# Node weights of a graph layer: slots of 16 outputs with both halves of the supports, in three bursts, for slots of 32 outputs with one half, in four periods

## The chip, the cores and the metric

The kernel runs on one core of one Trainium2 chip. The metric is the time of one execution on the device in microseconds. Before the change it is 1736.24 us, the median of three runs (1735.61 to 1749.89).

TensorE (PE) multiplies, and a weight load (PEld) goes before each matmul; its results go to PSUM[...]. VectorE (DVE) and ScalarE (ACT) read PSUM. [...]SyncE (SP) issues most DMA transfers, each engine in its own program order.

## The reference, cut to what matters

Four graph layers follow one another on x (8 batches, 2048 nodes, 64 features), each with a residual and a layernorm. The change is in the third, where every node has weights of its own, made from an embedding of 16 numbers:

```
support_set = [eye(N), lap, 2 * lap @ lap - eye(N), apt]         # lap is adj here
weights = einsum('nd,dkio->nkio', node_embeddings, weights_pool)  # 4 supports x 64 in x 64 out for every node
bias = node_embeddings @ bias_pool
x_g = einsum('knm,bmc->bknc', supports, x)                        # transposed to b, n, k, c
out = einsum('bnki,nkio->bno', x_g, weights) + bias
```

The fourth layer multiplies with adj again, three times.

## The kernel before, in words

Supports times x are formed first (`supports()`), transposed, and stored to DRAM as four terms: xt, u1, u2, u3. While they run, small jobs of the list `aside` are done one per tile step: among them 8 of the 16 adjacency tiles are written to `adj_hbm` (`keep_adj`), since their SBUF (`more0`, `more1`, 4 tiles or 4 MB each) is lent to the node weights; and the weight pool, split[...], is prepared as two stacks `wst[0]`, `wst[1]`, one for each half (two supports, 128 rows) of the contraction.

Then come the slots. A chunk is 256 nodes (8 chunks). For a chunk, `load_unit` brings two tiles `xg`, one for each half k: 1 MB as two DMAs (line 1440). A slot g stands for a chunk c, a half of the outputs (`hf`, 32 of 64), and one half k of the contraction: 32 slots, 4 for each chunk.

- `form(g, s)`, eight in a slot, forms weights of 4 outputs for all 256 nodes: four fp32r matmuls `pw<-est,wst`, 64 rows by 128 columns of the array in two row tiles, 256 columns moved. ACT copies `pw` out of a tile of two banks (even s, line 1512), or ACT and DVE each copy one bank (odd s, line 1516) into `w_half[k]`.
- `multiply(g - 1, v)`, four in a slot, takes the weights formed in the slot before: for 4 nodes at a time a weight load of 128 rows by 32 columns (8 batches of 4 nodes) and a product with 128 columns (4 nodes of 32 outputs), four column tiles side by side: 16 fp32 matmuls, each of which the profile shows as two passes with a weight load each. The result holds products of each node with each of four nodes; `pick` (lines 1520 and 1522, DVE) keeps the diagonal with a mask, four picks of 128x256 for each pair of periods, after both halves k have been added up in PSUM.

A slot has four periods: two forms, up to two picks, then one multiply. The order on every engine is written out by this loop (`pin`, `tc.keep_in_program_order`). PSUM in the slots: two product tiles `py` of two banks ("ph"), one forming tile of two banks ("two") and two of one bank ("one"). The first slot's forms are done among the last matmuls of `supports()` (`opening_forms`); in the last slot there are only multiplies, and the first work for the fourth layer.

`hooks` put other steps at (slot, period): loads of `est` and of `xg` (three buffers that rotate), and `chunk_end`, eight steps that end a chunk: store of the sums to `y_hbm` and loads of the residual (`store`, line 1558), loads of y turned (`load`, 1570), sum, squares, power and scale (POOL, ACT, DVE), store to `x3_hbm`.

After the slots the lent tiles come back from `adj_hbm`, the first four by POOL's queue and the other four by SP's, behind the last chunk's store and load. `opening()` does the first product of the fourth layer: tiles 0 to 6 first, then 7 to 11, then 12 to 15; the last chunk's end is done beside it, and `first_turn(3)` (transposes `pt`, line 175) waits for it. Line 172 is the helper `mm` that all matmuls have, so groups are told apart by their tiles.

Of the kernel before, what the change touches and what calls it, by code (L numbers as in the profile page):

```python
# [56 lines left out]
def tile_gnn_fast(  # L57
# [181 lines left out]
    terms = [dram.tile([NP * P, N], F32, name=f"{name}_hbm") for name in ("xt", "u1", "u2", "u3")]  # L239
    xt_hbm, u1_hbm, u2_hbm, u3_hbm = ([a[p * P:(p + 1) * P, :] for p in range(NP)] for a in terms)  # L240
    est_hbm = dram.tile([P, N], F32, name="est_hbm")
    adj_hbm = dram.tile([8, P, N], F32, name="adj_hbm")
    wst_hbm = dram.tile([P, F // 2, P], F32, name="wst_hbm")
    y_hbm = dram.tile([N // 256, F, B, 4, F], F32, name="y_hbm")
    xb_hbm = dram.tile([NP, P, NT, P], F32, name="xb_hbm")
# [11 lines left out]
    def column_halves(a):  # L257
        return [a[:, cols(g, N // 2)] for g in range(2)]

    def lent_tiles():  # L260

        tiles = []
        for i in range(2):
            more = adj_pool.tile([P, LENT // 2, N], F32R, tag=f"more{i}", name="adj_more")
            tiles += [column_halves(more[:, k, :]) for k in range(LENT // 2)]
        return tiles

    adj = [adj_tile(adj_pool, t) for t in range(LEND)] + lent_tiles()

    hrows = {}  # L270

# [163 lines left out]
    with tc.tile_pool(name="pa_ps", bufs=1, space=PSUM) as pps:  # L435
# [215 lines left out]
        adj += [adj_tile(adj_end, t) for t in range(NT - XT, NT)]  # L651

        fetch_rows(0)
        fetch_rows(1)
# [584 lines left out]
    def supports():  # L1239

        for p in range(NP):
            for k, hbm in ((1, u1_hbm), (2, u2_hbm)):
                chunks = [2, 3, 0, 1] if p == 0 and k == 1 else [*range(NCH)]
                uts = {}
                for g in range(2):
                    own = (2 * g, 2 * g + 1)
                    closing = (p, k, g) == (NP - 1, 2, 1)
                    if closing:
                        chunks = [1, 2, 0, 3]
                    ug = pph.tile([P, 2, C], F32, tag="ph", name="u", bufs=2)  # L1250
                    for q in chunks:
                        for t in range(q * JT, (q + 1) * JT):
                            for i in range(2):
                                for c in own:
                                    mm(
                                        ug[:, c % 2, :], lhsT=x_part[q][i][:, t % JT, :], rhs=adj_c(t, c),
                                        start=t == chunks[0] * JT and i == 0,
                                        stop=t == chunks[-1] * JT + JT - 1 and i == 1,
                                    )
                                    tick()  # L1260
                                    yield
                            if closing and q == 2 and t % JT == JT - 2:
# [138 lines left out]
    def second_stack():  # L1401
        for q in range(8):
# [44 lines left out]

    def bank(name):
        if wps is not None:
            return wps.tile([P, 2, Q], F32, tag="one", name=name, bufs=2).rearrange("p o n -> p (o n)")  # L1450
        return lps.tile([P, C], F32, tag="mm", name=name, bufs=4)

    def first_h(p, c, h, kept=lambda i: i):
# [24 lines left out]
        h[c] = first_h(0, c, l2.tile([P, C], F32, tag=f"g{c}", name=f"h{c}"))  # L1478
        later(n, lambda: factor(c, h[c], bd_e, None))

    H = F // 2
    w_half, w_four, scopes = [], [], {}
    opening_forms = [*range(8)]

    def lend(i):
        w_half.append(adj_pool.tile([P, Q, H], F32, tag=f"more{i}", name="w_half"))
        w_four.append(w_half[i].rearrange("p (m n) o -> p n m o", m=4))

    def begin_slots():
        nonlocal wps  # L1490
# [4 lines left out]

    picks = []

    def form(g, s):

        (c, hf), k = divmod(g // 2, 2), g % 2  # L1500
        if s % 2 == 0:
            pw = wps.tile([P, 2, 2, Q], F32, tag="two", name="pw", bufs=1)
            banks = [pw[:, j] for j in range(2)]
        else:
            banks = [wps.tile([P, 2, Q], F32, tag="one", name="pw", bufs=2) for _ in range(2)]
# [4 lines left out]
        dst = w_half[k][:, :, 4 * s:4 * s + 4]  # L1510
        if s % 2 == 0:
            pin(nc.scalar.copy(dst, pw.rearrange("p j o n -> p n (j o)")))  # L1512
        else:
            for j, (bank, eng) in enumerate(zip(banks, (nc.vector, nc.vector if k and s > 3 else nc.scalar))):
                copy = eng.tensor_copy if eng is nc.vector else eng.copy
                pin(copy(dst[:, :, 2 * j:2 * j + 2], bank.rearrange("p o n -> p n o")))  # L1516

    def pick(dst, src, m, first):
        if first:
# [4 lines left out]
    for _ in filler:  # L1524
        pass
    assert not aside and not opening_forms
    second_stack()
    lend(1)
    sums_2 = xnp.tile([P, 2, O4, F], F32, tag="xn2", name="sums_2")
    py = {}  # L1530

    def multiply(g, v):

        (c, hf), k = divmod(g // 2, 2), g % 2
        if v % 2 == 0 and k == 0:
            py[v] = pph.tile([P, 2, 4, 4, H], F32, tag="ph", name="py", bufs=2)
        both = py[v - v % 2]
        for i in range(4):
            for j in range(4):
                n = O4 * j + 4 * v + i  # L1540
                mm(
                    both[32 * j:32 * (j + 1), v % 2, i], lhsT=xg[2 * c + k][:, n], rhs=w_four[k][:, n],
                    start=k == 0 and i == 0, stop=k == 1 and i == 3,
                )
        if v % 2 and k:
            dst = sums_2[:, c % 2, 4 * v - 4:4 * v + 4, hf * H:(hf + 1) * H]
# [69 lines left out]
        at(4 * c - 2, 0, lambda c=c: load_est(c))  # L1616
    ends = [chunk_end(c) for c in range(UNITS // 2)]
    for c, stages in enumerate(ends[:-1]):
        for (slot, period), f in zip(((5, 2), (5, 3), (7, 0), (7, 2), (7, 3), (8, 0), (8, 1), (8, 2)), stages):
# [13 lines left out]
    for q in range(2):  # L1633
        at(SLOTS, 1 + q, lambda q=q: factor(q, h[q], bd_e, None, True))

    for g in range(1, SLOTS + 1):
        for period in range(4):
            for f in hooks.pop((g, period), ()):
                f()
            if 0 < g < SLOTS:  # L1640
                form(g, 2 * period)
                form(g, 2 * period + 1)
            for f in picks[:2]:
                f()
            del picks[:2]
            if g > 0:
                multiply(g - 1, period)
            if g == SLOTS:
                for f in picks:
                    f()  # L1650
                picks.clear()
    store, load, *waiting = ends[-1]
    adj[LEND:LEND + LENT] = lent_tiles()
# [12 lines left out]
    scopes["w"].close()  # L1666
# [958 lines left out]
```

## Time and profile before

| what | value |
|---|---|
| median of three runs | 1736.24 us |
| the profiled execution, as timed | 1743.63 us |
| its span in the profile | 1741.8 us |
| granted TensorE clock in it | 0.987 |
| node-weight slots in the span | 1017.8 to about 1254 us |

From the page (groups by line, engine and tiles; x is the count, then busy us in total and the mean ns of one, then idle time of the engine before them and what ended it):

```profile
L1516 DVE COPY w_half<-pw 128x512 f32<-128x512 f32 x160 | 109.7, 705 | 86.2 <-PE pw L172 85.4
L1512 ACT COPY w_half<-pw 128x1024 f32<-128x1024 f32 x128 | 129.9, 1015 | 56.9 <-PE pw L172 56.8
...
L172 PE MATMUL py<-w_half,xg 128*32 128x128 f32 x4096 | 142.2, 279 | 1.2 <-issue 1.2
...
L172 PEld LDWEIGHTS py<-w_half,xg 128*32 128x32 f32 x4096 | 111.3, 138 | 18.8 <-issue 1.9
...
L172 PE MATMUL pw<-est,wst 64*128 64x256 f32 x1024 | 110.0, 317 | 0.7 <-ACT w_half L1512 0.4
```

"128*32" is the part of the array that is used, rows by columns. `<-issue` is idle time for which the profile shows no producer. Matmuls overlap, so the mean of one is longer than the distance between two.

### The profile page before, as it was taken

To read this page: it belongs to the slowest core of one execution; us is meant where nothing else is said; L and a number is where in the kernel's file an instruction comes from. 1 tells how busy PE (TensorE), PEld (TensorE's weight loads), DVE (VectorE), ACT (ScalarE), POOL (GpSimd) and SP (SyncE) were. 2 spreads that over 40 slices of the span, in tenths; PEclk is the share of its full clock that TensorE was granted. 3 is DMA by queue.
4 is the path that set the end of the run, shared out by engine and by line. 5 is a ranking of instruction groups with operands and counts; after the bars stand their busy time and mean duration, and the time that the engine had idled before them with its cause. 6 is when DMAs were issued, how large, how long until landed. Compare 5 with 4: busy or idle time off the path is not lost. (4 is left out here: it accounts for less than half of the span.)

```text
span 1741.8 us, 27973 instructions
## 1 busy us (share of the span) xinstructions
PE 1659.0 (95%) x11196; PEld 1208.1 (69%) x11196; DVE 833.1 (48%) x1531; ACT 589.4 (34%) x1031; POOL 572.4 (33%) x515
## 2 busy tenths in 40 slices
PE   6889899999989999999999999999989999999996
PEld 4657666666664444468788878888767877878775
DVE  7678945677742221210127247777623433433332
ACT  1345533434322211112123267878512222212221
POOL 4578845566534444422023001322310200202001
PEclk9899999999999999999999999999999999999998
DMA  9744334444340000017344367575671121211211
GB/s 336 252 158 124 107 123 145 139 147 132 107 151 6 30 7 24 25 54 291 120 143 124 109 152 159 131 171 123 157 265 43 51 59 43 61 48 42 57 43 39
DMA packets 171180, 195.83 MB, mean 112 GB/s; under 512 B 71536, under 2 KB 116336, under 8 KB 169760
## 3 DMA queue, kind: packets, MB, share of 16 engines
q1 hardware_dynamic: 160096, 154.54, 30.5%
q0 software_dynamic: 8544, 30.68, 5.3%
q10 hardware_dynamic: 2400, 8.72, 1.3%
q8 instruction: 90, 1.47, 0.4%
q14 instruction: 50, 0.41, 0.1%
HBM read 126.72 MB, written 67.17 MB: 111 GB/s over the span
## 5 line engine op out<-in xcount | busy, mean ns | idle before, releaser
L172 PE MATMUL ua<-pt,xn 128*128 128x512 f32 x512 | 230.2, 592 | 1.4 <-DVE pt L1151 1.4
L172 PEld LDWEIGHTS ua<-pt,xn 128*128 128x128 f32 x512 | 96.9, 190 | 111.1 <-issue 104.0
L1516 DVE COPY w_half<-pw 128x512 f32<-128x512 f32 x160 | 109.7, 705 | 86.2 <-PE pw L172 85.4
L1512 ACT COPY w_half<-pw 128x1024 f32<-128x1024 f32 x128 | 129.9, 1015 | 56.9 <-PE pw L172 56.8
L172 PE MATMUL py<-w_half,xg 128*32 128x128 f32 x4096 | 142.2, 279 | 1.2 <-issue 1.2
L172 PE MATMUL u<-adj,v0h 128*128 128x512 f32 x384 | 134.5, 428 | 1.1 <-ACT h L1820 1.1
L172 PE MATMUL u<-adj_more,v2h 128*128 128x512 f32 x384 | 126.1, 406 | 0.0
L172 PE MATMUL u<-adj,v0l 128*128 128x512 f32 x384 | 125.0, 403 | 0.0
L172 PEld LDWEIGHTS py<-w_half,xg 128*32 128x32 f32 x4096 | 111.3, 138 | 18.8 <-issue 1.9
L172 PE MATMUL u<-adj_more,v2l 128*128 128x512 f32 x384 | 124.3, 401 | 0.0
L1157 POOL TENSOR_TENSOR acc<-acc,pt 128x512 f32<-128x512 f32 x60 | 76.5, 1274 | 104.3 <-DVE pt L1151 103.6
L172 PE MATMUL pw<-est,wst 64*128 64x256 f32 x1024 | 110.0, 317 | 0.7 <-ACT w_half L1512 0.4
L1151 DVE TENSOR_SCALAR pt<-pt 128x512 f32<-128x512 f32 x64 | 29.9, 466 | 152.4 <-ACT pt L1150 152.3
L172 PEld LDWEIGHTS pw<-est,wst 64*128 64x128 f32 x1024 | 82.2, 184 | 25.6 <-ACT w_half L1512 18.4
L1729 ACT CAST ar<-fcav 128x512 fp32r<-128x512 f32 x64 | 39.6, 618 | 168.9 <-DMA fcav<-in_adj_t 168.0
L1730 DVE SCALAR_TENSOR_TENSOR ar<-fcav,ar 128x512 f32<-128x512 f32 x64 | 45.8, 715 | 102.4 <-ACT ar L1729 102.4
L172 PE MATMUL u<-adj_more,v3l 128*128 128x512 f32 x288 | 93.1, 399 | 1.2 <-DVE v3l L168 1.2
L172 PE MATMUL u<-adj,v1h 128*128 128x512 f32 x288 | 93.7, 403 | 0.0
L1150 ACT ACTIVATE pt<-s 128x512 f32<-128x512 f32 x64 | 38.0, 598 | 164.5 <-PE s L172 164.5
L172 PE MATMUL u<-adj_more,v3h 128*128 128x512 f32 x288 | 92.7, 400 | 0.0
L172 PE MATMUL u<-adj,v1l 128*128 128x512 f32 x288 | 92.0, 397 | 0.0
L1701 POOL TENSOR_TENSOR x<-x,rows 128x512 f32<-128x512 f32 x16 | 22.5, 1430 | 211.4 <-PE pt L175 127.8
(408 smaller groups left out, 3275.7 us busy)
## 6 DMA issues: line engine op xcount, KB each, us to landing
fcav<-in_adj_t SPq DMA_DIRECT2D x64, 256.0 KB, 3.0
u_hbm<-ut SPq DMA_DIRECT2D x48, 256.0 KB, 3.7
xg<-u_hbm SPq DMA_DIRECT2D x24, 512.0 KB, 7.7
adj<-in_adj_t POOLq DMA_DIRECT2D x16, 512.0 KB, 7.8
adj_more<-in_adj_t POOLq DMA_DIRECT2D x16, 512.0 KB, 9.8
adj_hbm<-adj_more SPq DMA_DIRECT2D x16, 512.0 KB, 6.2
x_hbm<-r SPq DMA_DIRECT2D x28, 256.0 KB, 2.3
hs_hbm<-st ACTq DMA_DIRECT2D x8, 584.0 KB, 4.8
```

What stands on the lines that cost most here:

```text
L172: tc.keep_in_program_order(nc.tensor.matmul(*args, **kw))
L1150: nc.scalar.activation(pt, s, AF.Exp)
L1151: nc.vector.tensor_scalar(pt, pt, 1.0, None, op0=ALU.max)
L1157: nc.gpsimd.tensor_tensor(accs[c], accs[c], pt, ALU.add)
L1512: pin(nc.scalar.copy(dst, pw.rearrange("p j o n -> p n (j o)")))
L1516: pin(copy(dst[:, :, 2 * j:2 * j + 2], bank.rearrange("p o n -> p n o")))
L1701: nc.gpsimd.tensor_tensor(xs, xs, b2.to_broadcast([P, JT, P]), ALU.add)
L1729: nc.scalar.copy(ar, seen_a)
L1730: nc.vector.scalar_tensor_tensor(ar.bitcast(F32), seen_a, 1.0, ar.bitcast(F32), op0=ALU.mult, op1=ALU.not_equal, accum_out=left[:, t, k:k ...
```

## The change

A slot now stands for a chunk and a quarter of the outputs (16), and has both halves k. `form(g, s)`: s counts 0 to 7, k = s // 4. `w_half[g % 2]` holds both halves of one slot; forms of a slot write one of them and multiplies of the slot before read the other. `multiply(g - 1, v, k)` moves 64 columns (4 nodes of 16 outputs) and is called 8 times a slot for 4. A product tile is one bank ("one", two of them); forming tiles are of two banks, three in turn (`two_banks`: "two", and two of "ph"), and each is copied whole, six of eight by ACT, two by DVE. A slot has three bursts: 3 forms and 3 multiplies, 3 and 3, 2 and 2.

`xg` gets a fourth buffer, in the place of the last adjacency tile, so this tile is also kept in `adj_hbm` (9 tiles for 8) and comes back last. Loads of `xg` are put at slots 4c - 2 and 4c - 1 for 4c - 3 and 4c. The second weight stack is loaded in pieces during the closing pass of `supports()`, since the opening forms need both stacks. The first four lent tiles return at the beginning of the last slot, by SP's queue.

```diff
-    adj_hbm = dram.tile([8, P, N], F32, name="adj_hbm")
+    adj_hbm = dram.tile([9, P, N], F32, name="adj_hbm")
...
+                            if closing and t % JT == JT - 1 and q in (1, 2, 0):
+                                second_stack(range(2 * (1, 2, 0).index(q), 2 * (1, 2, 0).index(q) + 2))
...
-    for t in range(LEND, LEND + LENT):
+    for t in range(LEND, NT):
         for g in range(2):
             aside += [((0, 2), f) for f in [lambda t=t, g=g: keep_adj(t, g), *idle(1)]]
...
-        t = xnp.tile([P, B, Q], F32, tag=f"xn{(3, 0, 1)[u % 3]}", name="xg")
+        if u % 4 == 3:
+            t = adj_end.tile([P, B, Q], F32, tag="last", name="xg")
+        else:
+            t = xnp.tile([P, B, Q], F32, tag=f"xn{(3, 0, 1)[u % 4]}", name="xg")
...
-    H = F // 2
+    H = F // 4
...
-        w_half.append(adj_pool.tile([P, Q, H], F32, tag=f"more{i}", name="w_half"))
-        w_four.append(w_half[i].rearrange("p (m n) o -> p n m o", m=4))
+        w_half.append(adj_pool.tile([P, 2, Q, H], F32, tag=f"more{i}", name="w_half"))
+        w_four.append(w_half[i].rearrange("p k (m n) o -> p k n m o", m=4))
...
+    more_pw, turns = [], [0]
+
+    def two_banks():
+        turns[0] += 1
+        if turns[0] % 3:
+            return more_pw[turns[0] % 3 - 1]
+        return wps.tile([P, 2, 2, Q], F32, tag="two", name="pw", bufs=1)
+
     def form(g, s):
 
-        (c, hf), k = divmod(g // 2, 2), g % 2
-        if s % 2 == 0:
-            pw = wps.tile([P, 2, 2, Q], F32, tag="two", name="pw", bufs=1)
+        c, part_o = divmod(g, 4)
+        k, s = divmod(s, 4)
+        single = g == 0 and s % 2
+        if single:
+            banks = [wps.tile([P, 2, Q], F32, tag="one", name="pw", bufs=2) for _ in range(2)]
+        else:
+            pw = two_banks() if g else wps.tile([P, 2, 2, Q], F32, tag="two", name="pw", bufs=1)
             banks = [pw[:, j] for j in range(2)]
...
-            q, o = divmod(2 * (O4 // 2 * hf + s) + i, 4)
+            q, o = divmod(2 * (4 * part_o + s) + i, 4)
...
+            copy = nc.vector.tensor_copy if s == (1, 0)[k] and g > 0 else nc.scalar.copy
+            pin(copy(dst, pw.rearrange("p j o n -> p n (j o)")))
...
-    def multiply(g, v):
+    def multiply(g, v, k):
...
-            py[v] = pph.tile([P, 2, 4, 4, H], F32, tag="ph", name="py", bufs=2)
+            py[v] = wps.tile([P, 2, 4, 4, H], F32, tag="one", name="py", bufs=2)
...
-                    both[32 * j:32 * (j + 1), v % 2, i], lhsT=xg[2 * c + k][:, n], rhs=w_four[k][:, n],
-                    start=k == 0 and i == 0, stop=k == 1 and i == 3,
+                    both[32 * j:32 * (j + 1), v % 2, i], lhsT=xg[2 * c + k][:, n], rhs=w_four[g % 2][:, k, n],
+                    start=v % 2 == 0 and k == 0 and i == 0, stop=v % 2 == 1 and k == 1 and i == 3,
...
-        at(4 * c - 3 + 3 * k, 0, lambda u=u: load_unit(u))
+        at(4 * c - 2 + k, 1, lambda u=u: load_unit(u))
...
-        for period in range(4):
-            for f in hooks.pop((g, period), ()):
-                f()
-            if 0 < g < SLOTS:
-                form(g, 2 * period)
-                form(g, 2 * period + 1)
-            for f in picks[:2]:
-                f()
-            del picks[:2]
-            if g > 0:
-                multiply(g - 1, period)
...
+    def return_first():
+        adj[LEND:LEND + LENT // 2] = lent_tiles(0)
+        return_adj(range(LEND, LEND + LENT // 2), nc.sync)
+
+    at(SLOTS, 0, return_first)
+    bursts = ((0, 3), (3, 6), (6, 8))
...
+        for burst, (s0, s1) in enumerate(bursts):
+            for f in hooks.pop((g, burst), ()):
+                f()
+            some_picks(2)
+            if g < SLOTS:
+                for s in range(s0, s1):
+                    form(g, s)
+            some_picks(2)
+            for s in range(s0, s1):
+                multiply(g - 1, *divmod(s, 2))
...
-    return_adj(range(LEND, LEND + LENT // 2), nc.gpsimd)
     store()
     load()
-    return_adj(range(LEND + LENT // 2, LEND + LENT), nc.sync)
+    return_adj(range(LEND + LENT // 2, NT), nc.sync)
```

More of the change, by code (lines that the diff above doesn't have):

```diff
@@ L258, in column_halves, with lent_tiles, last_tile @@
         return [a[:, cols(g, N // 2)] for g in range(2)]
[L260 to L268, printed above, removed]
+    def lent_tiles(i):
+        more = adj_pool.tile([P, LENT // 2, N], F32R, tag=f"more{i}", name="adj_more")
+        return [column_halves(more[:, k, :]) for k in range(LENT // 2)]
+    def last_tile():
+        return column_halves(adj_end.tile([P, N], F32R, tag="last", name="adj_last"))
+    adj = [adj_tile(adj_pool, t) for t in range(LEND)] + lent_tiles(0) + lent_tiles(1)
     hrows = {}
@@ L650, in tile_gnn_fast @@
         adj_end = ctx.enter_context(tc.tile_pool(name="adj_end", bufs=1, side="right"))
-        adj += [adj_tile(adj_end, t) for t in range(NT - XT, NT)]
+        adj.append(last_tile())
         fetch_rows(0)
@@ L1399, in split_raw, with second_stack @@
         return [lambda i=i: rounded(i) for i in range(4)] + [lambda i=i: half(i) for i in range(4)]
-    def second_stack():
-        for q in range(8):
+    def second_stack(pieces):
+        for q in pieces:
             w = va.tile([P, 4, P], F32R, tag=f"v{(1, 1, 2, 2, 0, 0, 3, 3)[q]}{'hl'[q % 2]}", name="wst", bufs=1)
@@ L1449, in bank @@
         if wps is not None:
-            return wps.tile([P, 2, Q], F32, tag="one", name=name, bufs=2).rearrange("p o n -> p (o n)")
+            return two_banks()[:, 0].rearrange("p o n -> p (o n)")
         return lps.tile([P, C], F32, tag="mm", name=name, bufs=4)
@@ L1496, in tile_gnn_fast @@
     picks = []
-    def form(g, s):
-        (c, hf), k = divmod(g // 2, 2), g % 2
-        if s % 2 == 0:
-            pw = wps.tile([P, 2, 2, Q], F32, tag="two", name="pw", bufs=1)
+    more_pw, turns = [], [0]
[4 more added lines that the diff above has]
+        return wps.tile([P, 2, 2, Q], F32, tag="two", name="pw", bufs=1)
+    def form(g, s):
+        c, part_o = divmod(g, 4)
[5 more added lines that the diff above has]
+            pw = two_banks() if g else wps.tile([P, 2, 2, Q], F32, tag="two", name="pw", bufs=1)
             banks = [pw[:, j] for j in range(2)]
-        else:
-            banks = [wps.tile([P, 2, Q], F32, tag="one", name="pw", bufs=2) for _ in range(2)]
         for i in range(2):
-            q, o = divmod(2 * (O4 // 2 * hf + s) + i, 4)
+            q, o = divmod(2 * (4 * part_o + s) + i, 4)
             for j, r in enumerate(halves):
                 mm(banks[j][:, i, :], lhsT=wst[k][q][r, o, :], rhs=est[c][r, :], start=True, stop=True)
-        dst = w_half[k][:, :, 4 * s:4 * s + 4]
-        if s % 2 == 0:
-            pin(nc.scalar.copy(dst, pw.rearrange("p j o n -> p n (j o)")))
-        else:
-            for j, (bank, eng) in enumerate(zip(banks, (nc.vector, nc.vector if k and s > 3 else nc.scalar))):
-                copy = eng.tensor_copy if eng is nc.vector else eng.copy
-                pin(copy(dst[:, :, 2 * j:2 * j + 2], bank.rearrange("p o n -> p n o")))
+        dst = w_half[g % 2][:, k, :, 4 * s:4 * s + 4]
+        if single:
+            pin(nc.vector.tensor_copy(dst[:, :, 0:2], banks[0].rearrange("p o n -> p n o")))
+            pin(nc.scalar.copy(dst[:, :, 2:4], banks[1].rearrange("p o n -> p n o")))
+        else:
+            copy = nc.vector.tensor_copy if s == (1, 0)[k] and g > 0 else nc.scalar.copy
+            pin(copy(dst, pw.rearrange("p j o n -> p n (j o)")))
     def pick(dst, src, m, first):
@@ L1526, in tile_gnn_fast @@
     assert not aside and not opening_forms
-    second_stack()
+    second_stack(range(6, 8))
     lend(1)
+    more_pw += [pph.tile([P, 2, 2, Q], F32, tag="ph", name="pw", bufs=2) for _ in range(2)]
     sums_2 = xnp.tile([P, 2, O4, F], F32, tag="xn2", name="sums_2")
     py = {}
-    def multiply(g, v):
-        (c, hf), k = divmod(g // 2, 2), g % 2
+    def multiply(g, v, k):
+        c, part_o = divmod(g, 4)
         if v % 2 == 0 and k == 0:
-            py[v] = pph.tile([P, 2, 4, 4, H], F32, tag="ph", name="py", bufs=2)
+            py[v] = wps.tile([P, 2, 4, 4, H], F32, tag="one", name="py", bufs=2)
         both = py[v - v % 2]
@@ L1541, in multiply @@
                 mm(
-                    both[32 * j:32 * (j + 1), v % 2, i], lhsT=xg[2 * c + k][:, n], rhs=w_four[k][:, n],
-                    start=k == 0 and i == 0, stop=k == 1 and i == 3,
+                    both[32 * j:32 * (j + 1), v % 2, i], lhsT=xg[2 * c + k][:, n], rhs=w_four[g % 2][:, k, n],
+                    start=v % 2 == 0 and k == 0 and i == 0, stop=v % 2 == 1 and k == 1 and i == 3,
                 )
         if v % 2 and k:
-            dst = sums_2[:, c % 2, 4 * v - 4:4 * v + 4, hf * H:(hf + 1) * H]
+            dst = sums_2[:, c % 2, 4 * v - 4:4 * v + 4, part_o * H:(part_o + 1) * H]
             src = both.rearrange("p a i m o -> p (a i) m o")
@@ L1618, in tile_gnn_fast @@
     for c, stages in enumerate(ends[:-1]):
-        for (slot, period), f in zip(((5, 2), (5, 3), (7, 0), (7, 2), (7, 3), (8, 0), (8, 1), (8, 2)), stages):
+        for (slot, period), f in zip(((5, 1), (5, 2), (7, 0), (7, 1), (7, 2), (8, 0), (8, 1), (8, 2)), stages):
             at(4 * c + slot, period, f)
@@ L1634, in tile_gnn_fast @@
         at(SLOTS, 1 + q, lambda q=q: factor(q, h[q], bd_e, None, True))
-    for g in range(1, SLOTS + 1):
-        for period in range(4):
-            for f in hooks.pop((g, period), ()):
-                f()
-            if 0 < g < SLOTS:
-                form(g, 2 * period)
-                form(g, 2 * period + 1)
-            for f in picks[:2]:
-                f()
-            del picks[:2]
-            if g > 0:
-                multiply(g - 1, period)
[L1648 to L1653, printed above, removed]
     def return_adj(tiles, eng):
@@ L1658, in return_adj, with some_picks @@
                 pin(eng.dma_start(adj[t][g].bitcast(F32), adj_hbm[t - LEND, :, cols(g, N // 2)]))
-    return_adj(range(LEND, LEND + LENT // 2), nc.gpsimd)
+    def return_first():
[3 more added lines that the diff above has]
+    bursts = ((0, 3), (3, 6), (6, 8))
+    def some_picks(n):
+        for f in picks[:n]:
+            f()
+        del picks[:n]
+    for g in range(1, SLOTS + 1):
+        for burst, (s0, s1) in enumerate(bursts):
+            for f in hooks.pop((g, burst), ()):
+                f()
+            some_picks(2)
[5 more added lines that the diff above has]
+                multiply(g - 1, *divmod(s, 2))
+    some_picks(4)
+    assert not picks and not hooks
+    store, load, *waiting = ends[-1]
+    adj[LEND + LENT // 2:] = [*lent_tiles(1), last_tile()]
     store()
     load()
-    return_adj(range(LEND + LENT // 2, LEND + LENT), nc.sync)
+    return_adj(range(LEND + LENT // 2, NT), nc.sync)
     scopes["w"].close()
```

## The prediction

> **What bounds the kernel now.** I read the page first, then the windows of the node-weight stage, then the order of time inside it.
>
> ```profile
> span 1741.8 us, 27973 instructions
> ...
> PE 1659.0 (95%) x11196; PEld 1208.1 (69%) x11196; DVE 833.1 (48%) x1531; ACT 589.4 (34%) x1031; POOL 572.4 (33%) x515
> ...
> q8 instruction: 90, 1.47, 0.4%
> ```
>
> TensorE is busy 95%, so the time is its chain. The queue line becomes important below: 90 packets carry 1.47 MB, 16 KB each. There are 2 x 11196 loads and matmuls, about 250 for each packet, so this is TensorE's own instruction stream, one record per 64 bytes. The change is inside 1017.8 to 1246.3 us: 228.5 us, 31 slots that form and multiply, 7.37 us each.
>
> ```profile
> 1104.18 0.67 PEld L172 LDWEIGHTS pw<-est,wst 64*128 64x128 f32 x8 [0.17 <-ACT w_half L1512]
> 1104.18 0.87 PE L172 MATMUL pw<-est,wst 64*128 64x256 f32 x8
> ...
> 1104.78 1.01 ACT L1512 COPY w_half<-pw 128x1024 f32<-128x1024 f32 x1 [0.28 <-PE pw L172]
> 1104.98 0.86 PEld L172 LDWEIGHTS py<-w_half,xg 128*32 128x32 f32 x32
> ...
> 1104.98 1.11 PE L172 MATMUL py<-w_half,xg 128*32 128x128 f32 x32
> ...
> 1105.69 0.63 ACT L1516 COPY w_half<-pw 128x512 f32<-128x512 f32 x1
> ```
>
> This is the timeline of one quarter of a slot, 1.82 us. By the start times of the instructions: forms run 0.46 us when nothing holds them (a pair of row tiles every 0.118, the first 0.226), on average 0.58, since ACT frees the forming banks late; 0.206 from the last form to the first multiply; 0.834 for 32 multiply passes, four column tiles together every 0.109; 0.202 back. Sum 1.82. ACT copies 0.91 + 0.52 of each quarter (back-to-back starts). TensorE, its mode changes and ACT's copies close one loop.
>
> A second limit is close behind. The timeline of weight loads once shows
>
> ```profile
> 1225.60 0.85 PEld L172 LDWEIGHTS py<-w_half,xg 128*32 128x32 f32 x28
> 1227.87 0.20 PEld L172 LDWEIGHTS py<-w_half,xg 128*32 128x32 f32 x4 [1.42 <-issue]
> ```
>
> a stall in mid-burst for which the profile knows no producer. In the packet records of q8 a fetch starts at 1215.23, the next only at 1225.24 (1.34 us long), the next at 1228.92. Counting 256 instructions per packet from this one zero, TensorE has used up exactly all that was fetched (0 left) at 1226.42, and also at the other stalls: 1028.37, 1173.72, 1202.80. It resumes 1.29, 1.55, 1.25 and 1.41 us after a packet's end. Where instructions are used slowly (475 to 980 us, 1305 to 1709 us), every fetch starts with 273 to 301 left. So about 290 instructions are all the stock there is while a fetch is under way. And between 1226.6 and 1228.9 no fetch starts, though the DMA engines are idle:
>
> ```profile
> 1226.70:1227.70 1.00, 0.00 (x0) 0.00 (x0) 0.48 (x1) 0.21 (x1) 0.00 (x0) 1.00 0.10 24
> 1227.70:1228.80 1.10, 0.94 (x13) 0.73 (x12) 0.00 (x0) 0.00 (x0) 0.00 (x0) 1.00 0.05 14
> ```
>
> (windows; the last figures are clock, DMA share, GB/s). The next block is asked for after the last one is in use: one at a time.
>
> [...]the trace: a fetch whose stock passes 290 starts on average 2.46 us later (39 fetches, 0.66 to 5.11), the latest while x loads and y stores run.
>
> **The change part by part.**
>
> *Multiplies, 16 outputs of both halves.* The program's order of TensorE holds 4096 product matmuls for 2048, 64 columns for 128, the 1024 forms unchanged. An fp32 matmul is two passes, so 8192 weight loads and 8192 passes for 4096 each. A slot goes from 320 to 512 + 64 = 576 instructions. Streaming halves: estimate 0.055 us for a group of four, from 0.109; 64 groups a slot, 3.5 us as before. Bounds: 0.027 (four issues of 6.8 ns, the spacing inside a group) and 0.109 (no gain; see the rivals).
>
> *Bursts of three, three, two.* Three forms 0.226 + 4 x 0.118 = 0.70; change 0.206; 24 groups 23 x 0.0546 + 0.05 = 1.31; back about 0.17: 2.38 us. The burst of two: 0.46 + 0.206 + 0.87 + 0.17 = 1.71. Slot 6.47 us.
>
> *Copies.* Per slot ACT copies six tiles at 0.92 = 5.5 us, DVE two (1.2 to 1.38, from 0.69 for half) and 8 smaller picks (0.24 to 0.48, from 0.48 at twice the size), 4.3 to 6.6 us. With three forming tiles a form waits for the copy three before it. Laid out from the times above, only the third form of each slot does, 0.3 us: the last two copies of a slot are both ACT's. Slot **6.77 us** if instructions arrive. Product tiles of one bank are free before they are needed: picks follow one burst later.
>
> *Instructions.* At 6.77 us TensorE uses 85 a microsecond, 3.0 us per block. A block costs start + transfer + time until usable. Least: 1.06 (resume to next fetch, idle DMA) + 0.9 + 1.29 = 3.25 us. As this stage has it: 2.46 + 1.15 + 1.38 = 5.0 us. Both exceed 3.0, so fetching becomes the bound: 576/256 = 2.25 blocks a slot, 7.3 to 11.3 us. I take the middle, 4.13 us, 9.3 us a slot: the same bytes move over a longer time, and x loads lie apart from the y store. Then 31 x (9.3 - 7.37) = **+60 us**. The gains in changes and copies lie under this wait.
>
> *Last slot* (multiplies only, 8.1 us now): 512 + some 60 instructions, about 9 us, +1. *Opening forms* 4 to 7 read weight pieces that are loaded during the closing pass, behind 2 MB of x loads on SP's queue (landing 9.0 us for such a piece): 0 to 3 us, +1.
>
> *x loads.* Four buffers (the fourth is the last adjacency tile's), each pair of DMAs a slot apart, two to three slots ahead of use; landing 7.7 us is covered by a slot and more. The extra 1 MB write follows the sixteen others on SP (799 to 818 us); TensorE waits once, 2.3 us, between 560 and 1000 us, and nothing reads what is written before 1252. If SP's queue were late by these two landings (6.2 us each, overlapping), that would cost some 6 us once; I take nothing.
>
> *Return of the adjacency.* Eight DMAs (4 MB) move from POOL's queue after the slots to SP's at the last slot's start, ahead of the x3 store, the x load and the y store; 1 MB is added at the end. In 1254.4:1274.8 the DMA engines are full at 296 GB/s, and TensorE then waits 4.8 and 1.1 us for the y chain (PE pt, L175, <- DVE x, L1592), runs at half pace until 1286 (about 2.2 us) and waits 1.2 for v3l. Four MB at 296 GB/s are 14 us, started 6.4 us earlier: most of the 9 us goes. Against that y's store stands behind these DMAs, and the last five tiles' 5 MB (17 us) land about when the last one's pass comes: 0 to 5 us. I take -6 (-9 to +5). POOL loses 4.4 us of issuing that nobody waited for.
>
> **Sum.** +60 + 1 + 1 - 6 = +56. The profiled execution took 1743.6 us (span 1741.8), 0.4% over the median of 1736.2; the difference is carried over: **1792 us**.
>
> **The rivals.**
> 1. *Faster: instructions keep up.* [...]Against it: 0 left at four stalls, one fetch at a time. It decides where a block costs under 3.0 us: slot 6.77, 31 x -0.6 = -19, with +1 and -6: 1712. Break-even is a block at 3.3 us.
> 2. *Fetch-bound, but hardly any queueing*, the x loads being spread: 7.3 us a slot, -2 in all, -6 + 2: 1730, no change.
> 3. *Fetch waits as now*, 5.0 us a block: +120 - 4: 1852.
> 4. *Half-width passes gain nothing*, 0.109 a group: slot 6.47 + 3.5 = 9.97, +81: 1813. It decides from 0.095 us a group. For it: weight loads (median 137 ns) are as many per pass as before; against: four loads start within 20 ns of each other, so they run side by side.
>
> **How the numbers follow.** Fetch-bound between 7.8 and 11 us a slot 0.61, rival 1 0.17, rival 2 0.10, rival 3 0.05, rival 4 0.07. About 1% (17 us) is what can be told from no change. Faster 0.17, same 0.10, slower 0.73. The likeliest case's own range is 1745 to 1843. To leave no more than 2 in 10 out, 1720 to 1850: most of rival 1 stays outside below, a part of rival 3 above.
>
> **What would show it.** In the timeline of TensorE gaps "<-issue" of 1 to 3 us in most product bursts, two to three a slot, each ending about 1.3 us after a q8 packet; q8 near 122 packets (90 + 8192/256); ACT and DVE waiting for pw more than before; groups of four product passes at 0.055 us inside a burst. It is wrong if bursts run through (rival 1), or if groups come at 0.1 us (rival 4). For the opening: less than 2 us before L175's pt.

## The result, and the profile after

The changed kernel took 1832.06 us (median of six runs, 1825.21 to 1835.4) beside 1740.69 us for the kernel before on the same chip (six runs, the three above among them): a ratio of 1.0518, 95% interval 1.0501 to 1.0535. The profiled execution took 1825.21 us. The forecast was 1792 us, in a range of 1720 to 1850: the side and the mechanism were right, the size was 40 us short.

The page of the changed kernel, totals first, then groups (busy us in all, mean ns of one | idle before, what ended it):

```profile
span 1823.3 us, 36169 instructions
...
PE 1675.8 (92%) x15292; PEld 1233.3 (68%) x15292; DVE 830.1 (46%) x1565; ACT 595.8 (33%) x1001; POOL 567.9 (31%) x507
...
q8 instruction: 122, 2.00, 0.5%
...
L1531 ACT COPY w_half<-pw 128x1024 f32<-128x1024 f32 x190 | 182.5, 1022 | 142.3 <-PE pw L172 142.0
L172 PE MATMUL py<-w_half,xg 128*32 128x64 f32 x8192 | 168.5, 235 | 55.1 <-issue 54.9
L172 PEld LDWEIGHTS py<-w_half,xg 128*32 128x32 f32 x8192 | 148.0, 145 | 73.9 <-issue 62.3
```

TensorE's share falls from 95% to 92%. Before the product passes stood 1.2 us of idle time without a producer; now 54.9. ACT waits longer for TensorE's forms than before (142 us against 57), so ACT is not what holds the loop. The instruction queue has the 122 packets that were forecast: 32 more for 4096 more passes and 4096 more weight loads, 256 instructions to a packet.

The waits of TensorE in the 31 slots (us in all, times, longest):

```profile
PE py L172 <- issue: 52.0, 43, 5.3
PE pw L172 <- issue: 12.6, 5, 5.8
PE pw L172 <- DMA xg<-xt_hbm: 4.8, 1, 4.8
```

64.6 us are waits for nothing that the profile can name. They are waits for instructions. If the TensorE records are counted against 256 for each q8 packet, as in the prediction, all 48 of these waits end at the same count: all that was fetched is used up, and one new block has come. TensorE resumes 1.20 to 1.72 us after the end of that packet. The wait in the third line stands at this count too (one record off), 1.63 us after a packet's end at 1018.48, and ahead of a form, which reads no x tile. So it is most likely a wait for instructions as well, 69.4 us in all; the profile names the semaphore that came last.

Where the 81.5 us between the two spans lie, by the start times of the matmuls:

| part | before, us | after, us | difference | forecast |
|---|---|---|---|---|
| up to the first opening form | 1005.3 | 994.6 | -10.8 | 0 |
| opening forms | 12.5 | 15.9 | +3.4 | +1 |
| 31 slots that form and multiply | 228.5 | 316.5 | +88.0 | +60 |
| last slot | 8.1 | 11.4 | +3.3 | +1 |
| last product to the mixing product `pm` | 42.7 | 40.6 | -2.1 | -6 |

The first row is work that the change hardly touches, and it comes in small steps spread over the matmuls of the first 900 us. In the profiles of the runs built on the kernel before, that kernel's own among them, the first opening form starts at 998.9 to 1005.3 us; in those built on the changed kernel at 992.7 to 1002.3. It is taken as variation from execution to execution; whether some 5 us of it (the means are 1002.5 and 997.8) belong to the change stays open. The medians differ by 91 us where the spans differ by 82, since the profiled execution of the changed kernel was 6.9 us under its median and that of the kernel before 2.9 us over it.

To compare stretches that are alike, the experiments are read in slots 5 to 27 of each profile, from the first product pass of one to that of the other (a slot is counted here by the weights that it multiplies, 0 to 31). There the kernel before takes 7.30 us a slot, the changed kernel 10.60, and a block of 256 instructions (the distance from one q8 packet to the next) 5.80 and 4.65 us.

### The profile page after: what moved, and what is told of

The parts are those of the page before. It is cut to its first block, busy times and chain, and to the rows that moved or that the text cites. A ratio compares the mean times of both kernels' runs of the same rounds, so it can differ in the third digit from the quotient of the medians.

```text
span 1823.3 us, 36169 instructions
## 1 busy us (share of the span) xinstructions
PE 1675.8 (92%) x15292; PEld 1233.3 (68%) x15292; DVE 830.1 (46%) x1565; ACT 595.8 (33%) x1001; POOL 567.9 (31%) x507
## 4 chain that ended last, share of the span: by engine, by line
PE 73%; issue 6%; DMA 4%; DVE 3%; POOL 2%; ACT 2%; SPq 1%; POOLq 0%; ACTq 0%; DVEq 0%
PE u L172 37%; PE ua L172 12%; PE py L172 7%; PE pw L172 4%; PE ug L172 3%; PE pr L172 2%; PE pf L172 2%; PE po L172 1%; ACT w_half L1531 1%; PE pt L175 1%; PE s L172 1%; PE pd L172 1%; PE pi L172 1%; DMA x_hbm<-y 1%; DMA wst<-wst_hbm 1%
## 5 line engine op out<-in xcount | busy, mean ns | idle before, releaser
L1531 ACT COPY w_half<-pw 128x1024 f32<-128x1024 f32 x190 | 182.5, 1022 | 142.3 <-PE pw L172 142.0
L172 PE MATMUL py<-w_half,xg 128*32 128x64 f32 x8192 | 168.5, 235 | 55.1 <-issue 54.9
L172 PEld LDWEIGHTS py<-w_half,xg 128*32 128x32 f32 x8192 | 148.0, 145 | 73.9 <-issue 62.3
L172 PE MATMUL pw<-est,wst 64*128 64x256 f32 x1024 | 99.8, 317 | 21.3 <-issue 12.6
L1531 DVE COPY w_half<-pw 128x1024 f32<-128x1024 f32 x62 | 75.9, 1224 | 82.5 <-PE pw L172 82.4
L172 PEld LDWEIGHTS pw<-est,wst 64*128 64x128 f32 x1024 | 73.8, 198 | 37.8 <-issue 24.8
L172 PEld LDWEIGHTS u<-adj,v0h 128*128 128x128 f32 x384 | 70.3, 188 | 28.3 <-issue 13.2
## 6 DMA issues: line engine op xcount, KB each, us to landing
xg<-u_hbm SPq DMA_DIRECT2D x24, 512.0 KB, 10.4
```

The source lines that it names most:

```text
L172: tc.keep_in_program_order(nc.tensor.matmul(*args, **kw))
L1531: pin(copy(dst, pw.rearrange("p j o n -> p n (j o)")))
```

## The experiments

### Only more instructions: b_split, b_turns, b_half

b_split is the kernel before with every product cut into two of 64 columns. Nothing else of the change is in it.

```
+                for e in range(2):
+                    part = slice(e * H // 2, (e + 1) * H // 2)
-                    both[32 * j:32 * (j + 1), v % 2, i], lhsT=..., rhs=w_four[k][:, n],
+                        both[32 * j:32 * (j + 1), v % 2, i, :, part], lhsT=..., rhs=w_four[k][:, n, :, part],
```

> The kernel before, with each product matmul of the slots cut in two of 64 columns, nothing else moved: 576 instead of 320 instructions a slot, as in the changed kernel, with the same streaming, tiles, copies and loads. Theory (instructions arrive at 4.1 to 4.5 us per block of 256): 2.25 blocks make 9.3 to 10.2 us a slot instead of 7.37, so +60 to +88 us, about 1800 to 1828 us, with long waits for nothing that the profile shows (issue) inside the product bursts. Rival A (the new order of the work, its bursts, product tiles and copies cost the time): none of that is here, so within 10 us of the kernel before. Rival B (a pass of 64 columns costs as much as one of 128): 2048 more matmuls in groups of four at 0.109 us, +56 us, but evenly, without long waits.

1819.88 us, ratio 1.0459 (1.0424 to 1.0493); a slot 9.78 us, a block 4.35 us, q8 122 packets. More instructions alone bring most of the loss (79 of 91 us by the medians), and the new bursts, product tiles and copies are in none of it: rival A falls. An undisturbed burst takes 1.10 us, from 0.83, where rival B's full price would make it twice as long. The timeline of b_split's TensorE (start, us, what, count, idle before it) shows where:

```profile
1095.11 1.23 PE L172 MATMUL py<-w_half,xg 128*32 128x64 f32 x59
1099.92 0.64 PE L172 MATMUL py<-w_half,xg 128*32 128x64 f32 x5 [3.58 <-issue]
1100.49 1.22 PE L172 MATMUL pw<-est,wst 64*128 64x256 f32 x8
```

A burst stops after 59 of its 64 passes. Passes of one burst have the same producers and the same tiles, so neither a copy nor a load can stop it between the 59th and the 60th. All 29 of b_split's waits for "issue" in the slots end where the count of fetched instructions is out, as in the changed kernel.

In b_split both halves of a product follow each other on the same column tile, and an undisturbed burst takes 1.10 us. b_turns takes the column tiles in turn, as the changed kernel does:

```
-        for i in range(4):
+        for i in range(8):
+            i, e = divmod(i, 2)
```

> As the kernel before with every product cut in two (576 instructions a slot), but with the two halves apart, so that the four column tiles take turns as in the changed kernel, not two passes in a row on one tile. In the first cutting a burst of 64 passes took 1.105 us where the changed kernel's takes 0.956. Theory (the arrival of the instructions decides, a block of 256 every 4.39 us in the first cutting): no gain from quicker bursts, total within 10 us of the first cutting's 1819.9 us. Rival (part of its loss is passes in a row on one tile): 64 bursts' 0.15 us times four a slot are given back, 31 x 0.6 = 19 us, up to 38 us with the waits behind it: 1782 to 1801 us.

1815.61 us, ratio 1.0426 (1.0405 to 1.0447). An undisturbed burst takes 0.95 us instead of 1.10, and the total stays within 5 us of b_split's, with overlapping intervals (in slots 5 to 27 its profile is even slower, 10.09 us a slot against 9.78). Four bursts in each of 31 slots got quicker by 0.15 us, 19 us in all, and waits took the place of nearly all of it. That is what a bound on the arrival of instructions looks like.

b_half cuts only the products of every second period (`cuts = 2 if v % 2 else 1`), 448 instructions a slot.

> The kernel before, with only every second product block's matmuls cut in two: 448 instructions a slot. Theory (a block of 256 every 4.1 to 4.5 us is a floor, met where the TensorE is quicker): 1.75 blocks make 7.2 to 7.9 us, against 7.37 before, so 0 to +18 us, clearly less than half of what cutting all does. Rival A (order of the work): within 10 us. Rival B (a price per pass, no threshold): just half of what cutting all does, +30 to +44 us.

1784.89 us, ratio 1.0250 (1.0218 to 1.0283): +44 us, a little more than half of b_split. The theory as put there (a pace per block that is met or not) fails, and the rival gave this number. Its trace says why neither is right: a slot takes 8.77 us, of which undisturbed bursts would take 7.74 (two periods of each kind by their start times, 2 x 3.87). Most of the rest is stops of 1.4 to 2.8 us, one or two in a chunk, at the fetches that took 6 to 9 us while an x tile was loaded; the others take 3.4 to 5.2 us and stop nothing that matters. So the mean pace does not decide. Each single fetch is set against the stock of about 290 instructions (273 to 301 at the start of a fetch in the kernel before), and by estimate a stock used at 448/7.74 = 58 a microsecond lasts 5.0 us.

### The new order without the instructions: a_pairs

```
-        for i in range(4):
+        for i in (0, 2):
...
-                    both[..., v % 2, i], lhsT=xg[2 * c + k][:, n], rhs=w_four[g % 2][:, k, n],
+                    both[..., v % 2, i:i + 2], lhsT=xg[2 * c + k][:, n], rhs=w_four[g % 2][:, k, n:n + 2],
```

> The changed kernel with two neighbouring products made by one matmul of 128 columns, with the first one's x (so the second product is made from the wrong x: that part of the computation is changed): 320 instead of 576 instructions a slot, the same columns streamed, the same bursts, tiles, copies and loads. Theory: 1.25 blocks (5.2 to 5.7 us) no longer bound the slot, which falls from 10.21 us to TensorE's 6.3 to 7.0 us: -100 to -120 us, about 1712 to 1732 us, and the waits for nothing shown leave the bursts. Rival A (the new order of the work costs the time): the slot stays near 10 us and the total within 15 us of the changed kernel. Rival B (passes of 64 columns have a price of their own): the slot falls by 2 us to 8.2, about 1770 us.

1749.79 us, ratio 1.0071 (1.0038 to 1.0105), 82 us under the changed kernel: with 320 instructions a slot again, nearly all the loss is gone, and rivals A and B fall. But the forecast was 1712 to 1732. Most slots take 6.88 us, as laid out; one or two in each chunk take 7.5 to 11.3, and the waits in the slots are seven:

```profile
PE py L172 <- issue: 13.0, 7, 4.0
```

One stop in a chunk, each at a fetch of 8 to 12 us. The next experiments ask what that fetch meets.

### What a fetch waits for: a_noload, a_spread, a_quiet

In the changed kernel the x loads of a chunk are written a slot apart, but the timeline of SP's queue shows that they are issued at once:

```profile
1100.27 2.86 SPq L1586 DMA_DIRECT2D y<-y_hbm  x4
1103.17 0.62 SPq L1451 DMA_DIRECT2D est<-est_hbm  x1
1103.84 0.70 SPq L1445 DMA_DIRECT2D xg<-xt_hbm  x1
1104.58 2.72 SPq L1445 DMA_DIRECT2D xg<-u_hbm  x3
```

With four buffers nothing holds SP back, and it runs ahead of the slots: 2 MB in 3.5 us, right behind the turned y. (With three buffers, the kernel before had to wait for a tile to come free, and its two loads were 7 us apart.) The trace has this wait: SP waited 70.1 us for TensorE ahead of x loads in the kernel before (1030 to 1240 us), 5.5 us in the changed kernel (1050 to 1300 us). The loads of the three u terms land after 10.4 us in the median, 7.7 before. q8 starts a fetch at 1105.16 and the next at 1114.36, 9.2 us later, and TensorE stops:

```profile
1111.69 0.33 PE L172 MATMUL py<-w_half,xg 128*32 128x64 f32 x4
1117.15 2.78 PE L172 MATMUL py<-w_half,xg 128*32 128x64 f32 x92 [5.13 <-issue]
```

Each of the six chunks in these slots has one such fetch, 8.9 to 9.9 us from start to start; the others take 3.4 to 5 us. The packet itself takes no longer (1.39 us here): it is its start that comes late. Whether it waits in the queues of the DMA engines or in the memory behind them, no run separates.

a_noload reuses the x tiles of the first two chunks (`xg[u] = xg[u - 4]`):

> The changed kernel without the x loads of the third chunk on: the tiles of the first two chunks are used again, so these loads are left out and the products after them are made from old x. 576 instructions a slot as before. Theory (fetches are slowed by the data in the same DMA engines): the one fetch of 9 us in each chunk is gone, a block takes 3.7 to 4.0 us instead of 4.54, a slot 8.4 to 9.0 us: -38 to -55 us, 1777 to 1794 us; TensorE is still bound by instructions, some 1 us over the 7.1 us a slot that its bursts take unstalled. Rival (a fetch has a pace of its own, whatever data moves): within 10 us of the changed kernel.

1791.23 us, ratio 1.0294 (1.0262 to 1.0327), 8.80 us a slot, 3.90 a block: inside the theory's numbers. No wait in slots 5 to 27 is longer than 1.4 us.

a_spread keeps all loads, and gives them to ScalarE's queue:

```
-        at(4 * c - 2 + k, 1, lambda u=u: load_unit(u))
+        for i in range(2):
+            at(4 * c - 2 + k, 2 * i, lambda u=u, i=i: load_unit(u, (i,), nc.scalar))
```

> The changed kernel with its x loads issued by ScalarE's queue, which is paced by the copies, one half tile (512 KB) a burst or two apart instead of 2 MB in 3.5 us. Theory (the lump makes one fetch of 9 us, apart they make fetches of 5.5 to 6.5 us, as in the kernel before with its products cut): a block 4.3 to 4.45 us instead of 4.54, -5 to -18 us, 1814 to 1827 us. Rival (the bytes count, not their grouping): within 4 us of the changed kernel; or ScalarE, which now issues 16 loads of some 0.7 us, delays the forms: up to +10 us.

1818.16 us, ratio 1.0453 (1.0428 to 1.0479), 10.21 us a slot, 4.48 a block (4.3 to 4.45 forecast). The fetches of 9 us become several of 5 to 7; the gain is real but small, 14 us with the intervals apart. Net of what the other queue may cost, the lump is 0.39 us of a slot; that the bytes move at all is more.

a_quiet leaves out the x loads as a_noload does, and puts the stores and loads that end the first seven chunks into a heap ahead of the third last slot:

> The changed kernel without the x loads of the third chunk on, and with the stores and loads that end the first seven chunks put together ahead of the third last slot (so the sums they store are those of the last chunks, and old x is used): from slot 5 to slot 28 almost no data moves. Not the total is read here, which the heap of stores distorts, but the slots of the quiet stretch. Theory: a fetch that meets no data takes about 3.4 us (the shortest intervals seen elsewhere), so 2.25 blocks make 7.6 to 7.8 us a slot, against 7.1 us that the unstalled bursts take; instructions still bound it, by little. Rival (without data the fetch is quick enough): 7.1 us a slot and no waits; rival (the pace of 3.9 us seen without x loads is the fetch's own): 8.8 us a slot.

The total, 1893.49 us, isn't used. In the quiet stretch a slot takes 8.34 us and a block 3.70: midway between the theory's 7.6 to 7.8 and the second rival's 8.8, so both missed, and only the first rival (7.1 us and no waits) falls. The waits there (slots 5 to 27), and the windows of a_noload and a_quiet (the last figures are clock, DMA share, GB/s), in this order:

```profile
PE py L172 <- issue: 16.9, 26, 1.1
PE pw L172 <- issue: 2.3, 5, 0.7
```

```profile
1065.00:1215.00 150.00, 127.86 (x4948) 111.12 (x4944) 92.88 (x188) 104.14 (x114) 31.66 (x25) 1.00 0.28 64
```

```profile
1065.00:1215.00 150.00, 132.85 (x5169) 115.88 (x5170) 90.27 (x181) 103.21 (x108) 0.00 (x0) 1.00 0.03 9
```

With the DMA engines 3% busy TensorE still stops for instructions, shortly, 31 times in 49 blocks. So a fetch has a pace of its own, 3.7 us for 256 instructions in the mean (3.3 to 4.4), and data comes on top.

### The same questions with 320 instructions: b_traffic, a_pairs_spread, a_pairs_noload

b_traffic is the kernel before with a copy of 1 MB between two places of the chip's memory put on SP's queue behind the first x load of seven chunks.

> The kernel before, with 320 instructions a slot, and seven times 1 MB more of data moved between two places in the chip's memory, right behind the load of the first x tile of a chunk; nothing waits for it. The fetch that meets this x load takes 7.0 to 7.8 us in the kernel before, and the stock of about 290 instructions lasts 290/43 = 6.7 us. Theory (a fetch waits behind data in the same DMA engines, and TensorE stops when the stock is out): that fetch takes 10 to 12 us, TensorE stops 2.5 to 4 us seven times, +15 to +30 us. Rival (only the number of instructions counts, or a fetch has a pace of its own): within 4 us of the kernel before.

1772.03 us, ratio 1.0181 (1.0161 to 1.0201): +31 us, just above the upper end of what the theory said. It is no evidence for it: of the seven stops of 2.5 to 4 us for instructions there is none. The waits of TensorE and of ScalarE in its slots:

```profile
PE pw L172 <- ACT w_half L1513: 18.7, 8, 4.2
PE pw L172 <- issue: 2.2, 3, 0.9
```

```profile
ACT xb L1580 <- POOL y L1577: 19.1, 9, 4.2
```

At the first end of a chunk the loads of the turned y, behind the copy in SP's queue, were issued from 1062.85 us (1058.14 in the kernel before). POOL's first sum began at 1066.99 (1062.43); ScalarE stood for 3.55 us before a square (line 1580) with the copies of the forms queued behind it; TensorE waited 3.54 us for those. In slots 5 to 27 TensorE is idle for 0.94 us a slot more than in the kernel before, and 0.36 us longer busy, since the granted clock was halved for 20 us after these waits. A single total that fits would have passed for a proof.

a_pairs_spread puts the pairs and the spread loads together.

> The changed kernel with two neighbouring products by one matmul with the first one's x (320 instructions a slot; that part of the computation is changed) and with the x loads a burst or two apart on ScalarE's queue. It asks what the new order of the work is worth when neither the number of instructions nor the lump of loads is in the way. Theory: its bursts make 6.87 us a slot against 7.37 of the kernel before, and the waits of 1 to 4 us once a chunk (13 us in all with the lump) fall to some 3 us: -8 to -13 us against the lumped pairs' 1749.8 us, about 1737 to 1742 us. Rival (the waits there are not from the lump): within 4 us of 1749.8 us.

1755.69 us, ratio 1.0085 (1.0058 to 1.0112): not faster than with the lump, 8.15 us a slot. Here two fetches in a chunk take 7.3 to 10.3 us instead of one, and ScalarE waits 10.2 us for POOL's sums, which it doesn't do with the lump. Of the 0.65 us that a slot takes longer than with the lump, 0.16 is idle time of TensorE and 0.49 longer busy time: the granted clock was halved for 27 us of these slots, 7 us with the lump. So most of it is the slower clock after stops of 2.4 us and less; which of the two causes brought it stays open. Spreading the loads was no remedy.

a_pairs_noload was made after that miss, to see whether the stops of the pairs come from the x loads at all.

> The changed kernel with two neighbouring products by one matmul with the first one's x (320 instructions a slot) and without the x loads of the third chunk on (both parts of the computation are changed). Spreading the loads over ScalarE's queue had made the pairs slower (8.15 us a slot in slots 5 to 27, against 7.50 with the lump and 7.30 in the kernel before). Theory (the waits of the pairs are fetches behind x data, and ScalarE's issues and two slowed fetches in place of one cost more than the lump): slots of 6.88 to 7.0 us, -11 to -16 us against the lumped pairs' 1749.8 us, 1734 to 1739 us. Rival (they come from the other data, the loads and stores at the end of a chunk, or from the order of the work): slots of 7.3 us or more, 1745 us or more.

1729.75 us, ratio 0.9934 (0.9911 to 0.9957): 4 us under the theory's range, with its slots at the lower end of it. Slots 5 to 27 take 6.87 to 6.89 us, every one. The waits in its slots:

```profile
PE py L172 <- issue: 2.1, 1, 2.1
```

Seven stops, 13.0 us, become one, and that one lies in the first slots, where the loads are still there. So at 320 instructions a slot no fetch is too late without the x loads; whether they alone make it so, or together with the turned y loaded right ahead of them, isn't shown.

### A version that is 0.2% faster: b_early

b_early is the kernel before with one part of the change, the early return of four lent tiles:

```
+    def return_first():
+        adj[LEND:LEND + LENT // 2] = lent_tiles(0)
+        return_adj(range(LEND, LEND + LENT // 2), nc.sync)
+
+    at(SLOTS, 0, return_first)
```

> The kernel before, with the first four of the eight lent adjacency tiles read back by SP's queue at the start of the last slot instead of by GpSimd's queue after it, to see whether the wait at the opening of the last layer (42.7 us from the last product to the first mixing pass) holds anything that these reads cost. If the opening waits on them, -2 to -6 us; if it waits on the sums of the slots alone, within 1.5 us. Against it: 4 MB more beside the last slot's stores, up to +3 us.

1738.04 us, ratio 0.9983 (0.9973 to 0.9993). From the last product to `pm` it takes 39.2 us instead of 42.7, and the slots are as before (7.29 us). These are single profiles: in b_split, b_turns, b_half and b_traffic, which return the tiles as the kernel before does, the stretch takes 40.5 to 43.3 us, so b_early lies under all of them; in the runs built on the changed kernel, a_quiet apart, it takes 40.2 to 46.1, so there the gain doesn't show. The waits of TensorE in that stretch, of b_early and then of the changed kernel (the kernel before: 5.9 us for x in two waits, 1.2 us for v3l):

```profile
PE pt L175 <- DVE x L1589: 4.4, 2, 3.1
```

```profile
PE pt L175 <- DVE x L1608: 3.6, 2, 2.3
PE u L172 <- DVE v3l L168: 2.0, 1, 2.0
```

By the medians (22 and 28 runs) the part is worth about 3 us, 0.2%, inside the -2 to -6 forecast. It is the only part of the change that was run alone and gained.

## Why the prediction was right, and where it was short

The slots of the changed kernel can now be put together from measured steps (slots 5 to 27, us a slot):

| step | us a slot | of it TensorE busy | idle | from |
|---|---|---|---|---|
| kernel before | 7.30 | 7.29 | 0.01 | its profile |
| new bursts and copies, all instructions there | 7.08 | | | sum of the changed kernel's undisturbed bursts |
| a fetch's own pace, 3.70 a block | 8.34 | 7.42 | 0.92 | a_quiet |
| with the data that ends a chunk, 3.90 | 8.80 | 7.48 | 1.32 | a_noload |
| with the x loads, apart, 4.48 | 10.21 | 8.05 | 2.16 | a_spread |
| with the x loads in a lump, 4.65 | 10.60 | 8.04 | 2.57 | the changed kernel |

Each row is one profile, and b_split and b_turns, whose fetches meet the same loads, differ by 0.31 us a slot (9.78 and 10.09). The steps of 0.39 and 0.46 are little more than that; for the lump the medians stand beside it.

*The bound.* "Both exceed 3.0, so fetching becomes the bound" held. b_split has the loss without the new order, a_pairs has the new order without the loss, and b_turns makes the bursts quicker without a gain. The stops in mid-burst, the 122 packets and the longer waits of ACT and DVE came as listed.

*The cost of a block: the term that was mis-sized.* "I take the middle, 4.13 us": it was 10.21/2.25 = 4.54 us over all 31 slots. That is +88 where +60 stood, and 28 of the 37 us by which the sum of +56 was short of what the stage and the opening became (+92.6). The reason given for the middle had two halves. "The same bytes move over a longer time" was true and helped less than thought: even with the kernel before's own loads (b_split) a block took 4.35. "x loads lie apart" was false: a hook in a later slot sets the place of a load in SP's queue, and in the kernel before it was the wait for a buffer that set the time; with the fourth buffer this wait was gone (70.1 us of waits ahead of x loads, 5.5 after). By a_spread this is 0.39 us a slot, some 12 us in all. The lower bound was too low as well: 3.25 us was summed from the best of each part, and an undisturbed fetch takes 3.70. Of the three parts in its sum, the transfer (1.15 us in the changed kernel) and the time until usable (1.41) were right. The start is the part that moved: from the end of a stop to the next fetch it takes 1.25 us in a_quiet, 1.43 in a_noload and 2.38 in the changed kernel, where the sum had 1.06 at the least.

*The bursts.* Groups of four passes came every 0.059 us inside undisturbed bursts (96 passes in 1.43 us), 0.055 forecast; the undisturbed slot is 7.08 us, 6.77 forecast. It lies under the fetches, as the prediction said, so the difference did not show. Rival 4 (0.109 a group) falls on it.

*What was not in the sum.* The trace shows the granted clock around the stop of 5.13 us above (windows of the changed kernel: busy time of each engine, clock, DMA share, GB/s):

```profile
1108.60:1112.00 3.40, 3.33 (x99) 2.61 (x90) 1.37 (x3) 2.60 (x3) 0.00 (x0) 1.00 1.16 210
1112.00:1117.10 5.10, 0.03 (x2) 0.00 (x0) 1.13 (x3) 1.78 (x3) 0.00 (x0) 0.73 0.88 157
1117.10:1119.80 2.70, 2.65 (x92) 2.54 (x91) 0.00 (x0) 0.00 (x0) 0.00 (x0) 0.50 0.03 6
1119.80:1121.50 1.70, 1.70 (x23) 1.49 (x24) 0.37 (x1) 0.74 (x1) 0.00 (x0) 0.59 0.00 0
```

After the stop TensorE runs at half clock for some 4 us: 92 passes take 2.78 us instead of 1.37 (96 take 1.43 undisturbed). In the clock records of the changed kernel's slots each stretch at 0.5 is 3.4 or 6.8 us long; in b_half the clock fell after stops of 1.9 to 2.8 us. Slots 5 to 27 of a_noload, a_spread and the changed kernel, in this order:

```profile
1058.80:1252.40 193.60, 164.53 (x6341) 143.11 (x6339) 119.26 (x243) 132.71 (x145) 43.67 (x33) 1.00 0.29 66
1059.00:1283.50 224.50, 177.07 (x6338) 154.85 (x6336) 119.64 (x243) 133.16 (x145) 43.40 (x33) 0.91 0.56 114
1059.50:1292.90 233.40, 176.92 (x6343) 154.32 (x6341) 119.31 (x243) 133.05 (x145) 43.47 (x33) 0.90 0.53 108
```

The figure after the comma is TensorE's busy time; divided by 22 slots it gives the table. Of the 1.41 us that the x loads bring when they lie apart, 0.84 are stops and 0.57 longer busy time, at a mean clock of 0.91; the lump's 0.39 are stops alone. Whether a full clock would give the 0.57 back isn't shown. At half clock TensorE used 92 passes and 91 weight loads in 2.78 us, 66 instructions a microsecond, and 256 in 3.70 us are 69, so by this estimate it might only stop sooner at full clock.

*The small terms.* Opening forms +3.4 for +1 (a wait of 2.0 us for `wst`, as named, and 0.8 for ACT's `ut`). Last slot +3.3 for +1: 2.9 us of it are two waits for "issue". The last layer's opening -2.1 for -6, inside the bounds given, and less than profiles of this stretch vary; that L175 would wait less than 2 us was wrong (3.6 us). The sum of these three is +4.6 for -4.

*The rivals.* 1 (instructions keep up) and 2 (hardly any queueing, 7.3 us a slot) fall: 8.34 us is what a slot costs with the DMA engines 3% busy, and no q8 packet of the two kernels (90 and 122) starts less than 2.1 us after the end of the one before it. Rival 3 (5.0 us a block, 1852 us) lies 20 us above the result, the forecast 40 below it. In giving 0.05 to it and taking the middle, the queueing was judged too kindly.

## What to carry to other kernels

Where TensorE is given many small matmuls, count its instructions by the microsecond: here 44 a microsecond (320 in 7.30 us) could be kept up with but for 1.5 us of stops, 47 (320 in 6.88 us) not while 2 MB were loaded in a lump, 58 not while a tile of 1 MB was loaded, and 81 (576 in 7.08 us) never. Wider matmuls (a_pairs, 82 us less than the changed kernel), not quicker ones (b_turns, 4 us less than b_split, with overlapping intervals), were the remedy, and a bulk load is set against how long the stock of instructions lasts, fetch by fetch. A step placed later in the program need not be later in time: here two pairs of x loads a slot apart were issued within 3.5 us, since the added buffer had taken away the wait of their queue.

## What the runs showed of the hardware

- A fetch of 256 instructions takes 3.70 us from one to the next with the DMA engines 3% busy, 3.90 with 28%, and 8.9 to 9.9 us behind 2 MB of loads (a_quiet, a_noload, the changed kernel). It is the start that comes late: the packet takes 1.08 us in a_quiet and 1.15 in the changed kernel.
- When the fetched instructions are out, TensorE stops, in mid-burst too (after 59 of 64 passes in b_split), and resumes 1.2 to 1.7 us after the end of the next packet (48 waits of the changed kernel). In the profile this is idle time with "issue", and once it was put down to a transfer.
- Twice the number of product passes of half the width is streamed nearly as quickly as forecast (0.059 us for four, from 0.109; 0.055 forecast), and the kernel is still 5% slower.
- With instructions and loads out of the way the new order is worth 0.42 us a slot (6.88 against 7.30, a_pairs_noload; the kernel before keeps its x loads, with 1.5 us of stops in 1030 to 1240 us). With the instructions and loads that it has, the change loses 3.30 us a slot instead.
- After stops the granted clock was 0.50 for 3.4 or 6.8 us at a time; in the changed kernel 92 passes then took 2.78 us instead of 1.37. At 320 instructions a slot this was most of what spreading the loads cost (0.49 of 0.65 us).
